# Projections and feed-forward products in four column tiles of the array

## The chip, the cores and the metric

The kernel runs on one core of a Trainium2 chip. The metric is device time in microseconds (us) per execution, taken as the median of several runs. All runs quoted here were fast, with a mean granted clock between 0.96 and 0.98. Two kernels that run in the same rounds on the same chip are compared by a ratio: the mean time of one kernel's fast runs over that of the other's of the same rounds, with a 95% interval, so it is not quite the ratio of the medians that stand beside it.

Engines in the profile are PE (TensorE matmul), PEld (TensorE weight load), DVE (VectorE), ACT (ScalarE), POOL (GpSimd) and SP (SyncE).

## The reference

Sixteen graphs of 1024 nodes with 128 features share one adjacency matrix. Each graph passes three transformer layers whose attention is masked by that matrix, and then one graph-attention layer. Everything is fp32. Cut to one layer:

```python
q, k, v = h @ Wq, h @ Wk, h @ Wv              # 8 heads of 16
s = einsum("bhqd,bhkd->bhqk", q, k) / 4
p = softmax(where(adj, s, -inf)) @ v
x1 = layer_norm(h + p @ Wo + bo)              # ln1
h  = layer_norm(x1 + relu(x1 @ W1 + b1) @ W2 + b2)   # ln2, W1 128x256, W2 256x128
```

## The kernel before

The unit of work is a block: one graph in one layer, 48 in all. A block is a row of 32 steps. In each step TensorE computes the scores of four heads for 128 keys and 512 queries, then the products of older exponentials with v, then at most one "piece" of other work: a transpose (T), a projection, or a feed-forward product. The order on TensorE is fixed by the program. The order on ACT, DVE and POOL is made by a scheduler when the program is built.

```python
def slot():   # scores: 3 x 2 banks of PSUM
    return psum.tile([P, N], dtype, tag="s", name="s", bufs=3)
def bank():   # every piece: one bank
    return psum.tile([P, 512], F32, tag="t", name="t", bufs=1)
sums = psum.tile([P, 512], F32, tag="acc", name="acc", bufs=1)   # products with v: one bank
...
def project(lhs, rhs, h, out):            # Wv, Wo, W2: N=128
    ps = bank()
    for t in range(4):
        for f in range(len(lhs)):
            nc.tensor.matmul(ps[:, t * P:(t + 1) * P], lhs[f][:, t * P:(t + 1) * P], rhs[f],
                             start=(f == 0), stop=(f == len(lhs) - 1))
    out(slice(4 * h, 4 * h + 4), ps)
...
def run():                                # split(): Wk, Wq, N=512
    ps = bank()
    nc.tensor.matmul(ps, w[n], s["xT", h], start=True, stop=True)
    with soon():
        nc.scalar.copy(hi[:, c], ps)
        nc.vector.tensor_sub(lo[:, c], ps, hi[:, c].bitcast(F32))
...
def run():                                # ffn1(): W1, N=512
    ps = bank()
    nc.tensor.matmul(ps, w["W1"][:, f * P:(f + 1) * P], s["x1T", h], start=True, stop=True)
    with soon():
        nc.scalar.activation(s["h", f, h], ps, AF.Relu, bias=w["b1"][:, f:f + 1], scale=1.0)
...
def score_step(step):                     # two pairs of heads
    for pp in range(2):
        ...                               # two row tiles, 64 rows each, into slot()
        on_pool = pp == 0 and kt not in BOTH_ON_DVE
        if on_pool:
            nc.scalar.activation(ev, psv, AF.Exp, scale=HD ** -0.5)
            nc.gpsimd.tensor_mul(ev, ev, m)
        else:
            nc.vector.tensor_add(ev, psv, m)
            nc.scalar.activation(ev, ev, AF.Exp, scale=HD ** -0.5)   # in place
...
def av_step(step, e, acc, first, last):   # four column tiles of 32, 17 columns used in each
    for j in range(J):
        nc.tensor.matmul(acc[j * SLOT:j * SLOT + HD + 1, :], v_bufs[m % 2][:, kt, 2 * j + g, :], e[:, j, :],
                         start=first, stop=last)
```

All eight PSUM banks are taken (six for scores, one for sums, one for pieces). Each piece must be copied out of its one bank, mostly by ACT, before the next piece may begin. ACT has two exponentials in each step besides.

Of the kernel before, what the change touches and what calls it, by code (L numbers as in the profile page):

```python
# [18 lines left out]
P = 128  # L19
# [4 lines left out]
SLOT = 32  # L24
# [24 lines left out]
def gnn_stack(tc: tile.TileContext, a: dict, out: bass.AP):  # L49


    nc = tc.nc
    with tc.tile_pool(name="flag", bufs=1) as fp:
        flag = fp.tile([1, 1], I32, name="flag")
        fast_path(tc, a, out, flag)
        bad = nc.values_load(flag[0:1, 0:1], min_val=0, max_val=1024)  # L56
        with tc.If(bad > 0):
            general_path(tc, a, out)
# [48 lines left out]
def fast_path(ctx: ExitStack, tc: tile.TileContext, a: dict, out: bass.AP, flag):  # L107
    nc = tc.nc
# [16 lines left out]
    def bank():  # L125

        return psum.tile([P, 512], F32, tag="t", name="t", bufs=1)

    def half_tile(name):

        return work.tile([P, 512], F32, tag="w", name=name, bufs=TILES["w"])
# [113 lines left out]
    for i in range(2):  # L245
        t = const.tile([P, NT, H, HD + 1], F32, name=f"v{i}")
# [4 lines left out]
    def soon():  # L251

        return tc.high_priority(offset=SOON)

    def transpose_half(name, src, h, gain=None, bias=None):

        dst = half_tile(name)
        ps = bank()
        for t in range(4):
            nc.tensor.transpose(ps[:, t * P:(t + 1) * P], src[:, 4 * h + t, :], identf)  # L260
        with soon():
            if gain is None:
                nc.scalar.copy(dst, ps)
            else:
                nc.scalar.activation(dst, ps, AF.Identity, scale=gain, bias=bias)
        return dst

    def v3(ps):
        return ps.rearrange("p (t d) -> p t d", d=D)

    def rows(v, n=NT):
        return v[:, None, :].to_broadcast([P, n, D])

    def project(lhs, rhs, h, out):

        ps = bank()
        for t in range(4):
            for f in range(len(lhs)):
                nc.tensor.matmul(ps[:, t * P:(t + 1) * P], lhs[f][:, t * P:(t + 1) * P], rhs[f],  # L279
                                 start=(f == 0), stop=(f == len(lhs) - 1))  # L280
        out(slice(4 * h, 4 * h + 4), ps)

    def with_stats(x):

        return (x, work.tile([P, NT, 6], F32, tag="st", name="st", bufs=4),
                work.tile([P, NT, 2], F32, tag="mv", name="mv", bufs=4))
# [8 lines left out]
    def add_and_stats(n):  # L295
        def out(ts, ps):
            with soon():
                nc.vector.tensor_add(n[0][:, ts, :], v3(ps), n[0][:, ts, :])  # L298
            stats(n, ts)
        return out  # L300

    def normalise(n, ts):

        z, _, mv = n
        m, v = mv[:, ts, 0], mv[:, ts, 1]
        nc.gpsimd.tensor_scalar(m, m, -1.0, None, op0=OP.mult)  # L306
        nc.gpsimd.tensor_scalar(v, v, EPS, None, op0=OP.add)
        nc.gpsimd.tensor_tensor(v, v, half_neg[:, ts], OP.pow)  # L308
        for t in range(ts.start, ts.stop):
            nc.gpsimd.tensor_scalar(z[:, t, :], z[:, t, :], mv[:, t, 0:1], mv[:, t, 1:2], op0=OP.add, op1=OP.mult)  # L310

    def scale_shift(z, gain, bias):
        n = z.shape[1]
        nc.gpsimd.tensor_mul(z, z, rows(gain, n))  # L314
        nc.gpsimd.tensor_add(z, z, rows(bias, n))  # L315
# [3 lines left out]
    def check_range(r):  # L319

        for k, op in enumerate((OP.min, OP.max)):
            nc.vector.tensor_reduce(chk[:, k, checks[0]:checks[0] + 1].bitcast(I32), r.bitcast(I32), AX.X, op)
        checks[0] += 1


    def proj_tasks(m):
        b, l = blocks[m]
        w = W[l]
        s = {}

        def t0(h):
            def run():
                x = state["x", b]
                if l == 0:
                    s["xT", h] = transpose_half("xT", x, h)
                    if h == 1:
                        nc.gpsimd.tensor_add(x, x, rows(w["bo"]))
                else:

                    s["xT", h] = transpose_half("xT", x, h, W[l - 1]["ln2_gc"], W[l - 1]["ln2_bc"])  # L340
                    if h == 1:
                        scale_shift(x, W[l - 1]["ln2_g"], w["bo"])
            return run

        def split(n, h):
            def run():
                if h == 0:
                    state[n, m] = [work.tile([P, N], F32R, tag="hl", name=i, bufs=4) for i in ("hi", "lo")]
                hi, lo = state[n, m]
                c = slice(h * 512, (h + 1) * 512)  # L350
                ps = bank()
                nc.tensor.matmul(ps, w[n], s["xT", h], start=True, stop=True)
                with soon():
                    nc.scalar.copy(hi[:, c], ps)
                    nc.vector.tensor_sub(lo[:, c], ps, hi[:, c].bitcast(F32))  # L355
            return run

        def v(h):
            def out(ts, ps):
                with soon():  # L360
                    nc.scalar.copy(v_bufs[m % 2][:, ts].rearrange("p t h s -> p (t h) s")[:, :, :HD],
                                   ps.rearrange("p (m d) -> p m d", d=HD))
            return lambda: project([s["xT", h]], [w["Wv"]], h, out)

        pieces = [t0(0), t0(1), split("Wk", 0), split("Wk", 1), split("Wq", 0), split("Wq", 1), v(0), v(1)]
        return [(2 if n in (3, 4, 5, 6) else 1, f, {0: "+w", 1: "+w", 6: "-w", 7: "-w"}.get(n, "")) for n, f in enumerate(pieces)]
# [59 lines left out]
    def post_tasks(b, l):  # L426
        w = W[l]
        s = {}
        att, recs = state["A"], state["recs"]

        def gather(h):
            def run():
                s["aT", h] = half_tile("aT")
                nc.vector.transpose(s["aT", h], att[:, h].rearrange("p k g d -> p (k g d)"))
                if h == 1:
                    check_range(recs.rearrange("p g h k -> p (g h k)"))
            return run

        def out_proj(h):
            def run():  # L440
                if h == 0:
                    s["n1"] = with_stats(state["x", b])
                project([s["aT", h]], [w["Wo"]], h, add_and_stats(s["n1"]))
                normalise(s["n1"], slice(4 * h, 4 * h + 4))
            return run

        def x1t(h, alone=False):
            def run():
                x1 = s["n1"][0]
                s["x1T", h] = transpose_half("x1T", x1, h, w["ln1_gc"], w["ln1_bc"])  # L450
                if alone:
                    scale_shift(x1[:, 4 * h:4 * h + 4, :], w["ln1_g"], w["b2"])
                elif h == 1:
                    scale_shift(x1, w["ln1_g"], w["b2"])
            return run

        def ffn1(f, h):
            def run():
                s["h", f, h] = half_tile("hT")
                ps = bank()  # L460
                nc.tensor.matmul(ps, w["W1"][:, f * P:(f + 1) * P], s["x1T", h], start=True, stop=True)  # L461
                with soon():
                    nc.scalar.activation(s["h", f, h], ps, AF.Relu, bias=w["b1"][:, f:f + 1], scale=1.0)  # L463
            return run

        def ffn2(h):
            def run():
                if h == 0:
                    s["n2"] = with_stats(state["x", b])
                project([s["h", f, h] for f in range(NF)], [w["W2"][:, f, :] for f in range(NF)], h,  # L470
                        add_and_stats(s["n2"]))
                normalise(s["n2"], slice(4 * h, 4 * h + 4))
            return run

        def both():
            gather(0)()
            gather(1)()


        together = [(2, both, "+w +w"), (1, out_proj(0), "-w"), (1, out_proj(1), "-w"), (5, x1t(0), "+w"), (1, x1t(1), "+w")]  # L480
        for h in range(2):
            together += [(1, ffn1(0, h), "+w"), (1, ffn1(1, h), "+w -w")]
        together += [(1, ffn2(0), "-w -w"), (1, ffn2(1), "-w -w")]
        alone = [[(1, gather(h), "+w"), (1, out_proj(h), "-w"), (3, x1t(h, True), "+w"), (1, ffn1(0, h), "+w"),
                  (1, ffn1(1, h), "+w -w"), (1, ffn2(h), "-w -w")] for h in range(2)]
        return together, alone
# [211 lines left out]
    n = 0  # L698
# [47 lines left out]
    ps = bank()  # L746
# [226 lines left out]
```

## Time and profile before

| | before |
|---|---|
| median of 3 runs | 4299.87 us (4289.3 to 4303.16) |
| profiled span, clock | 4307.9 us, 0.974 |
| busy: PE, DVE, ACT, POOL | 93%, 79%, 79%, 80% |
| matmul records | 26069 (an fp32 product has two) |
| an ordinary block | 77.45 us |
| a block beside a graph's last layer | 84 to 109 us |

"An ordinary block" is measured from the first scores of a block to those of the next. In a timeline, a bracket is idle time and what ended it.

The prediction shows the page's lines and TensorE's timeline. Two further views matter. The first is the timeline of ACT in the kernel before, over the two steps whose TensorE rows the prediction shows (start in us, duration, line, operation, operands; a bracket is idle time and what ended it):

```profile
3654.59 1.05 ACT L401 ACTIVATE e<-e 128x1024 f32<-128x1024 f32 x1
3655.54 1.01 ACT L397 ACTIVATE e<-s 128x1024 f32<-128x1024 f32 x1
3656.44 1.06 ACT L401 ACTIVATE e<-e 128x1024 f32<-128x1024 f32 x1
3657.39 0.69 ACT L463 ACTIVATE hT<-t,b 128x512 f32<-128x512 f32 x1
```

The piece of L461 that began at 3655.54 leaves its bank through the copy hT at L463. Between that piece and its copy, ACT runs exponentials 0.90 to 0.95 us apart, and the copy ends at about 3658.1. TensorE wants the bank again at 3658.24, when the next piece begins. The copy is hidden, with little to spare.

The second view is the list of waits of the kernel before (waiter, released by, total us, times, longest us):

```profile
PEld s L390 <- ACT e L397: 202.8, 242, 1.7
...
PE s L390 <- ACT e L397: 54.8, 120, 1.4
```

Scores wait for the exponential that reads their PSUM slot. A wait of PEld may be hidden behind a matmul that still runs; a wait of PE is idle time.

### The profile page before, as it was taken

How to read it: one execution, taken by the hardware profiler on the slowest of the kernel's cores; microseconds unless marked ns; L12 is line 12 of the kernel's file. 1: busy time of each engine (PE TensorE's matmuls, PEld its weight loads, DVE VectorE, ACT ScalarE, POOL GpSimd, SP SyncE). 2: the span in 40 equal slices, each digit the busy share in tenths (PEclk: the TensorE clock that was granted, in tenths of full speed). 3: DMA queues.
4: the chain of work that ended last, by engine and by line, in shares of the span. 5: the costliest groups of instructions: out<-in, count | busy, mean ns of one | idle time of the engine just before them, and what ended most of it. 6: DMA issues, size and time to landing. Idle time of an engine off the chain costs nothing. (4 is left out here: it accounts for less than half of the span.)

```text
span 4307.9 us, 70734 instructions
## 1 busy us (share of the span) xinstructions
PE 4005.4 (93%) x26069; PEld 1631.7 (38%) x26069; DVE 3408.0 (79%) x5324; ACT 3408.3 (79%) x3961; POOL 3442.0 (80%) x3010
## 2 busy tenths in 40 slices
PE   7999999999999999999999999999999999999996
PEld 2333333344443333334444333333344433333445
DVE  6888878877777888877777787887777788888774
ACT  7898989866767988987676898997776689898660
POOL 4788888876779888887677988887777788888784
PEclk9999999999999999999999999999999999999997
DMA  5222122221111222121112222221211212221100
GB/s 145 64 60 54 49 57 59 58 52 50 43 50 47 60 59 52 49 58 50 50 43 57 56 51 53 60 59 40 60 46 45 64 40 60 59 55 44 45 21 17
DMA packets 126147, 230.77 MB, mean 54 GB/s; under 512 B 36705, under 2 KB 75617, under 8 KB 125793
## 3 DMA queue, kind: packets, MB, share of 16 engines
q1 hardware_dynamic: 122896, 225.14, 20.9%
q8 instruction: 209, 3.42, 0.3%
q10 hardware_dynamic: 2896, 1.01, 0.1%
q14 instruction: 146, 1.19, 0.1%
HBM read 15.54 MB, written 8.39 MB: 6 GB/s over the span
## 5 line engine op out<-in xcount | busy, mean ns | idle before, releaser
L400 DVE TENSOR_TENSOR e<-s,mask_add 128x1024 f32<-128x1024 f32 x2112 | 2503.1, 1212 | 505.6 <-PE s L390 393.0
L401 ACT ACTIVATE e<-e 128x1024 f32<-128x1024 f32 x2112 | 2194.4, 1060 | 428.9 <-DVE e L400 415.3
L398 POOL TENSOR_TENSOR e<-e,mask 128x1024 f32<-128x1024 f32 x960 | 2047.3, 2145 | 470.2 <-ACT e L397 454.2
L407 PE MATMUL acc<-e,v 128*17 128x512 f32 x12288 | 1645.0, 607 | 44.9 <-POOL e L398 32.0
L390 PE MATMUL s<-Wq,Wk 64*128 64x512 f32 x6144 | 1217.0, 461 | 126.5 <-ACT e L397 54.8
L397 ACT ACTIVATE e<-s 128x1024 f32<-128x1024 f32 x960 | 979.8, 1021 | 137.8 <-PE s L390 73.6
L390 PEld LDWEIGHTS s<-Wq,Wk 64*128 64x128 f32 x6144 | 500.6, 186 | 1036.9 <-DVE e L400 330.9
L407 PEld LDWEIGHTS acc<-e,v 128*17 128x17 f32 x12288 | 206.5, 95 | 559.7 <-issue 440.6
L310 POOL TENSOR_SCALAR x<-x,mv 128x128 f32<-128x128 f32 x896 | 389.2, 447 | 22.7
L314 POOL TENSOR_TENSOR x<-x,ln_g 128x1024 f32<-128x1024 f32 (+1 forms) x97 | 228.8, 2359 | 129.8 <-PE t L260 118.9
L576 PEld LDWEIGHTS t<-hd,e 128*128 128x128 f32 x2048 | 259.3, 208 | 67.2 <-issue 31.8
L576 PE MATMUL t<-hd,e 128*128 128x129 f32 x2048 | 271.4, 295 | 7.8 <-DVE x L582 3.5
L308 POOL TENSOR_TENSOR mv<-mv,half_neg 128x4 f32<-128x4 f32 x224 | 232.0, 1036 | 18.3
L298 DVE TENSOR_TENSOR x<-t,x 128x512 f32<-128x512 f32 x192 | 132.1, 688 | 123.3 <-PE t L279 118.9
L461 PE MATMUL t<-x1T,W 128*128 128x512 f32 x384 | 217.7, 649 | 5.1 <-DVE x L582 1.0
L279 PEld LDWEIGHTS t<-W,hT 128*128 128x128 f32 x1536 | 183.9, 196 | 88.0 <-ACT hT L463 35.8
L279 PE MATMUL t<-W,hT 128*128 128x128 f32 x1536 | 202.5, 286 | 3.4 <-DVE lo L355 2.4
L291 DVE BATCH_NORM_STATS2 st<-x 128x6 f32<-128x128 f32 x896 | 197.3, 279 | 2.7
L260 PE MATMUL t<-identf,x 128*128 128x128 f32 x896 | 151.8, 294 | 36.5 <-DVE lo L355 25.5
L260 PEld LDWEIGHTS t<-identf,x 128*128 128x128 f32 x896 | 97.1, 144 | 230.7 <-DVE lo L355 55.8
L306 POOL TENSOR_SCALAR mv<-mv 128x4 f32<-128x4 f32 x224 | 52.8, 236 | 140.0 <-DVE mv L293 101.8
L463 ACT ACTIVATE hT<-t,b 128x512 f32<-128x512 f32 x192 | 132.2, 688 | 40.8 <-PE t L461 40.0
(83 smaller groups left out, 2588.0 us busy)
## 6 DMA issues: line engine op xcount, KB each, us to landing
Wk<-hi SPq DMA_DIRECT2D x384, 128.0 KB
Wk<-lo SPq DMA_DIRECT2D x384, 128.0 KB
Wq<-hi SPq DMA_DIRECT2D x384, 128.0 KB
Wq<-lo SPq DMA_DIRECT2D x384, 128.0 KB
x<-in_x_dram SPq DMA_DIRECT2D x16, 512.0 KB
out_dram<-x SPq DMA_DIRECT2D x31, 256.0 KB
ai<-in_adj_dram SPq DMA_DIRECT2D x8, 512.0 KB
g_rows<-parts SPq DMA_DIRECT2D x124, 4.0 KB
```

The costliest lines, as they stand in the source:

```text
L260: nc.tensor.transpose(ps[:, t * P:(t + 1) * P], src[:, 4 * h + t, :], identf)
L279: nc.tensor.matmul(ps[:, t * P:(t + 1) * P], lhs[f][:, t * P:(t + 1) * P], rhs[f], start=(f == 0), stop=(f == len(lhs) - 1))
L308: nc.gpsimd.tensor_tensor(v, v, half_neg[:, ts], OP.pow)
L310: nc.gpsimd.tensor_scalar(z[:, t, :], z[:, t, :], mv[:, t, 0:1], mv[:, t, 1:2], op0=OP.add, op1=OP.mult)
L314: nc.gpsimd.tensor_mul(z, z, rows(gain, n))
L390: nc.tensor.matmul(ps[:, r * 512:(r + 1) * 512], k[64 * r:64 * r + 64, kt * P:(kt + 1) * P], q[64 * r:64 * r + 64, q0:q0 + 512], start=Tru ...
L397: nc.scalar.activation(ev, psv, AF.Exp, scale=HD ** -0.5)
L398: nc.gpsimd.tensor_mul(ev, ev, m)
L400: nc.vector.tensor_add(ev, psv, m)
L401: nc.scalar.activation(ev, ev, AF.Exp, scale=HD ** -0.5)
L407: nc.tensor.matmul(acc[j * SLOT:j * SLOT + HD + 1, :], v_bufs[m % 2][:, kt, 2 * j + g, :], e[:, j, :], start=first, stop=last)
L576: nc.tensor.matmul(ps[:, i * (D + 1):(i + 1) * (D + 1)], e[:, t, i * P:(i + 1) * P], s["hd"][t // 4][:, t % 4, :], start=(t == 0), stop=(t ...
```

## The change

Scores use two row tiles of the array, products with v use four column tiles, and pieces used the whole array. The change gives the pieces the shape of the products with v that stand ahead of them, so that one change of shape per piece falls away. It costs three more matmul instructions for each one split. Nothing else in the program text changes.

```diff
+    def by_columns(dst, lhsT, rhs, start=True, stop=True):
+        for j in range(0, P, SLOT):
+            nc.tensor.matmul(dst[j:j + SLOT, :], lhsT[:, j:j + SLOT], rhs, start=start, stop=stop)
@@ project
-                nc.tensor.matmul(ps[:, t * P:(t + 1) * P], lhs[f][:, t * P:(t + 1) * P], rhs[f],
-                                 start=(f == 0), stop=(f == len(lhs) - 1))
+                by_columns(ps[:, t * P:(t + 1) * P], lhs[f][:, t * P:(t + 1) * P], rhs[f],
+                           start=(f == 0), stop=(f == len(lhs) - 1))
@@ split
-                nc.tensor.matmul(ps, w[n], s["xT", h], start=True, stop=True)
+                by_columns(ps, w[n], s["xT", h])
@@ ffn1
-                nc.tensor.matmul(ps, w["W1"][:, f * P:(f + 1) * P], s["x1T", h], start=True, stop=True)
+                by_columns(ps, w["W1"][:, f * P:(f + 1) * P], s["x1T", h])
```

## The prediction

> **What bounds the kernel now.** I read four views, in this order: the page (busy shares and costliest groups), the timeline of TensorE over a few steps, the table of busy time by stretch, and the waits.
>
> The page first: its first line, and rows of the costliest groups (line, engine, operation, shapes, count | busy us, mean ns | idle before).
>
> ```profile
> PE 4005.4 (93%) x26069; PEld 1631.7 (38%) x26069; DVE 3408.0 (79%) x5324; ACT 3408.3 (79%) x3961; POOL 3442.0 (80%) x3010
> ...
> L407 PE MATMUL acc<-e,v 128*17 128x512 f32 x12288 | 1645.0, 607 | 44.9 <-POOL e L398 32.0
> L390 PE MATMUL s<-Wq,Wk 64*128 64x512 f32 x6144 | 1217.0, 461 | 126.5 <-ACT e L397 54.8
> ...
> L461 PE MATMUL t<-x1T,W 128*128 128x512 f32 x384 | 217.7, 649 | 5.1 <-DVE x L582 1.0
> L279 PE MATMUL t<-W,hT 128*128 128x128 f32 x1536 | 202.5, 286 | 3.4 <-DVE lo L355 2.4
> ```
>
> TensorE is busy 93% and the others about 80%. Its stationary shapes are the point: scores are 64*128 (two row tiles), products with v are 128*17 (four column tiles), projections and feed-forward are 128*128 (whole array). One step of the loop is scores, then products with v, then at most one "piece" (a projection, a feed-forward product or a transpose). Every fp32 product has two records, so eight records at L407 are four products. The timeline shows one step after the other (start, duration, records):
>
> ```profile
> 3655.54 1.12 PE L461 MATMUL t<-x1T,W 128*128 128x512 f32 x2
> 3656.60 0.73 PE L390 MATMUL s<-Wq,Wk 64*128 64x512 f32 x4
> 3657.26 1.05 PE L407 MATMUL acc<-e,v 128*17 128x512 f32 x8
> 3658.24 1.12 PE L461 MATMUL t<-x1T,W 128*128 128x512 f32 x2
> 3659.30 0.73 PE L390 MATMUL s<-Wq,Wk 64*128 64x512 f32 x4
> 3659.96 1.05 PE L407 MATMUL acc<-e,v 128*17 128x512 f32 x8
> 3660.94 2.05 PE L279 MATMUL t<-W,hT 128*128 128x128 f32 x16
> 3662.93 0.74 PE L390 MATMUL s<-Wq,Wk 64*128 64x512 f32 x4
> ...
> 4190.78 1.91 PE L407 MATMUL acc<-e,v 128*17 128x512 f32 x16
> 4192.62 0.74 PE L564 MATMUL s<-g_rows,h_rows 4*128 4x256 f32 x8
> ```
>
> Read starts, not durations (ends are modelled). No brackets follow these rows: TensorE waits for nobody. Products with v and an L461 piece take 3656.60 - 3654.56 = 2.04 us together (the L407 before the first row starts at 3654.56). At 4190 the trace has the one place where two groups of products with v follow each other: 1.84 us, although both pairs stream the same columns. The 0.20 us is what changing the shape of the array costs. In the single records (starts a few ns apart) it is two terms: after the last L407 matmul the next shape starts 522 ns later, where the two rounds of the double group are 429 ns apart, so about 95 ns of emptying; and the first weight load of the new shape is exposed, some 107 ns (the first L279 matmul to the second is 214 ns, later ones 112).
>
> The table by stretch, for the 77 us of one block in a part without the last layer:
>
> ```profile
> 3591.00:3614.00 23.00, 21.35 (x146) 6.08 (x145) 22.50 (x34) 22.61 (x24) 21.06 (x21) 1.00 0.36 92
> 3614.00:3668.00 54.00, 52.23 (x336) 20.11 (x335) 42.31 (x65) 47.08 (x55) 45.47 (x36) 1.00 0.17 40
> ```
>
> Columns: PE, PEld, DVE, ACT, POOL busy. In the 23 us without pieces ACT (98%) and DVE bind; in the 54 us with pieces TensorE does (97%), ACT is at 87%. All changed work lies in the second stretch, so there a saving on TensorE counts.
>
> **What the Trainium skill says.** "TensorEngine Tiling (Array Packing)", Key Properties: changing the tiling mode, not merely the tile, drains TensorE, and different tiles load weights and multiply in parallel. The trace agrees: 95 ns between shapes, none in the double group. Same page, Restrictions: column tiling excludes Fast Weight Load. "TensorE: Matmul & The Clock Gate", Weight-path perf modes, says that load is not used for fp32, so nothing is lost here. The latter page, Part 1, gives a floor of about 25 ns between matmul starts. Four column tiles at N=128 need one start per 27 ns, close to it. The trace shows L407 tiles starting 6 to 7 ns apart, which speaks for no such limit between tiles, though only for bursts of eight.
>
> **The change, part by part.** Each 128*128 product becomes four 128*32 ones writing four quarters of the output partitions, all streaming the same operand. Removed: one change of shape per piece. Added: from 3072 records at L279 and 768 at L352 and L461 three times as many again, 11520 more matmuls and as many loads (26069 becomes 37589). Moved: nothing in the data flow; transposes, scores and L524, L576 stay.
>
> N=512 pieces: now 2.04 us from the products with v to the next scores, then as the double group 1.84: -0.20. N=128, eight records: now 2.07 (products with v start at 1066.98, the next scores at 1069.05); then two rounds of 429 ns, eight rounds of 112 ns (four tiles at once, so a round lasts as long as one matmul now), 20 ns of stagger, 98 ns of emptying: 1.87, again -0.20. Sixteen records: now 2.97 (3659.96 to 3662.93), then 858 + 16 x 112 + 118 = 2.77: -0.20. The change back to scores stays in all.
>
> Number of pieces, from the page's counts: L279 with Wv 768/8 = 96, with Wo 96, with W2 1536/16 = 96, L352 384/2 = 192, L461 192: 672. 672 x 0.20 = **134 us** of TensorE.
>
> What comes off it:
> - Pieces that wait anyway. The waits list DVE lo 74.1 us in 45 times and several ACT and DVE waits before L279 and L461; I take 90 pieces as late, where emptying was hidden and about 0.12 us is lost: -11.
> - The instruction order of both kernels shows that the scheduler, which counts in instructions, moves PSUM copies on ACT: of 672 or so, about 120 stand one exponential later (48 of 96 v copies, 30 x1T, 28 xT), 30 one earlier. One exponential is about 0.95 us, and there is one bank for all pieces, needed again after about 1.65 us. I estimate 0.15 us of new wait for 90 net cases: -13.
> - ACT goes from 87% to 47.08/51.3 = 92% in the stretch with pieces, so some of the gain is lost to its queue, an estimate: -10.
>
> 134 - 34 = 100 us: 4300 - 100 = **4200 us**, 2.3% less.
>
> **The rivals.**
> 1. Small products don't keep the pace. If a round of four at N=128 took 150 ns instead of 112 (weight loads of four tiles in a row, 4 x 27 ns, or issue), the 384 groups of eight rounds would pay 384 x 8 x 38 ns = 117 us, and the change would be a wash, about 4310. At 200 ns a round it would be 4450. For it: 64 or 128 instructions must pass in 0.9 or 1.8 us where now it is 16 or 32. Against it: the loads in the double group start 1 to 2 ns after the matmul ahead of them and are hidden, and 32 columns load faster than 128 (L407 loads of 17 columns show 95 ns, of 128 columns 190). About 12%.
> 2. ACT and DVE take over as the bound. In the stretch without pieces they already do; if ACT held every piece step, with two exponentials (1.9 us) and a copy (0.6) against TensorE's new 2.50, half of the gain would stay: 4235. For it: 98% in the first stretch. Against it: not every piece has a copy on ACT, and steps in the last-layer phases, where ACT is near 70%, run at TensorE's pace too.
> 3. Full gain with 107 ns rounds (the streaming time of 128 fp32 columns, 427/4) instead of 112: 384 x 8 x 5 ns = 15 us more, nothing lost elsewhere: 4150.
>
> **Range and chances.** Rival 1 makes the upper tail, rival 2 puts weight between 4215 and 4250, rival 3 ends the lower side. The 2% line is 4214. Range 4150 to 4265; faster 0.63, same 0.32, slower 0.05.
>
> **What would show it.** Right: products with v to scores over an L461 piece at 1.84 us, over eight-round pieces near 1.87, over sixteen-round near 2.77; 37589 matmul records; TensorE's wait for ACT and DVE up some 20 to 40 us; the stretch with pieces some 2.5 us shorter per block, the one without unchanged. Wrong: rounds of small products well above 112 ns (rival 1), new idle time before pieces or scores put down to ACT copies (rival 2), or a remaining gap between products with v and pieces, which would mean that 17 and 32 columns are not one shape.

## More of the kernel before

By the trace, 22 of the 48 blocks take 77.2 to 77.8 us, most of them 77.45. Most of the others run beside the graph-attention layer of a graph that has just finished.

## The result, and the profile after

The changed kernel is correct and takes 4254.32 us (4 runs, 4250.95 to 4260.73) against 4301.51 us of the kernel before (4 runs, 4289.3 to 4308.17). The ratio is 0.9895, interval 0.987 to 0.9921: 1.05% faster, or 47 us. The forecast gain was 100 us.

The page of the changed kernel, its first line and three rows of the costliest groups:

```profile
PE 3892.9 (92%) x37589; PEld 1575.2 (37%) x37589; DVE 3404.9 (80%) x5324; ACT 3417.3 (80%) x3961; POOL 3451.4 (81%) x3010
...
L412 PE MATMUL acc<-e,v 128*17 128x512 f32 x12288 | 1635.4, 604 | 56.5 <-DVE tt L423 29.8
...
L271 PE MATMUL t<-x1T,W 128*32 128x512 f32 x1536 | 206.2, 609 | 18.0 <-ACT hT L468 8.6
...
L271 PE MATMUL t<-W,hT 128*32 128x128 f32 x6144 | 187.1, 274 | 9.1 <-DVE x L303 5.2
```

The pieces are now of shape 128*32, with four times the records, 37589 in all as forecast. TensorE is busy 112 us less. The idle time just before the W1 pieces went from 5.1 us to 18.0. That is the first sign that the pieces now come sooner than their bank is free.

From the single records, the span between the last product with v and the next scores fell where nobody waits as follows. With N=512 it fell from 1578 ns to 1381, with eight rounds (Wv and Wo) from 1610 to 1396, and with sixteen (W2) from 2504 to 2269. The gap from products with v to the piece went from 522 ns to 409, and the first weight load of the piece is hidden. Multiplied by 384, 192 and 96 pieces, that is 75.6 + 41.1 + 22.6 = **139 us** that TensorE no longer needs, or 2.9 us per block. So the part that was to happen on TensorE did happen, a little better than the 134 us forecast.

The table of busy time by stretch of the changed kernel (PE, PEld, DVE, ACT, POOL busy), over the same block that the prediction shows of before:

```profile
3547.50:3570.50 23.00, 21.55 (x152) 6.17 (x152) 22.48 (x32) 22.27 (x24) 21.61 (x21) 1.00 0.39 93
3570.50:3624.20 53.70, 50.49 (x580) 19.26 (x572) 42.33 (x66) 47.78 (x55) 45.23 (x36) 1.00 0.16 41
```

The stretch without pieces is unchanged at 23 us. The stretch with pieces is 53.7 us long where it was 54.0, although TensorE's busy time in it fell by 1.7 us and TensorE needs 2.9 us less. An ordinary block takes 77.15 us where it took 77.45. So the ordinary blocks give back nearly all of their gain: 22 x 0.30, about 7 us of the 47, where TensorE's need fell by 22 x 2.9 = 64. The other blocks gave the rest (two of them: 102.03 to 98.40, and 103.23 to 98.46).

Two rows of the waits of the changed kernel, those that answer to the ones shown of before:

```profile
PEld s L395 <- ACT e L402: 237.2, 313, 1.5
...
PE s L395 <- ACT e L402: 67.9, 138, 0.9
```

TensorE's waits for the exponentials grew. Counted over the whole trace as the time between matmul starts beyond the smallest spacing of its kind, all waits of TensorE grew from 480 to 566 us, while the sum of smallest spacings fell by 140. A second count of the records finds the same growth of 86 us; 56 of it lie before pieces and transposes, 19 before products with v.

Where this happens is best seen in two places of the same ordinary block. The first is the steps of W1. TensorE's timeline in the changed kernel:

```profile
3612.37 1.04 PE L271 MATMUL t<-x1T,W 128*32 128x512 f32 x8
3613.34 0.74 PE L395 MATMUL s<-Wq,Wk 64*128 64x512 f32 x4
3614.01 1.05 PE L412 MATMUL acc<-e,v 128*17 128x512 f32 x8
3615.28 1.06 PE L271 MATMUL t<-x1T,W 128*32 128x512 f32 x8 [0.21 <-ACT hT L468]
```

ACT's timeline over the same step:

```profile
3611.74 1.05 ACT L406 ACTIVATE e<-e 128x1024 f32<-128x1024 f32 x1
3612.69 1.01 ACT L402 ACTIVATE e<-s 128x1024 f32<-128x1024 f32 x1
3613.59 1.05 ACT L406 ACTIVATE e<-e 128x1024 f32<-128x1024 f32 x1
3614.54 0.68 ACT L468 ACTIVATE hT<-t,b 128x512 f32<-128x512 f32 x1
```

ACT does what it did before: exponentials 0.90 to 0.95 us apart, then the copy, which begins 2.17 us after its piece here and 1.85 us in the rows of before. The piece of 3612.37 could be followed by the next after 2.50 us, at 3614.87, but its copy begins at 3614.54 and ends past 3615.1. So the next piece begins at 3615.28 and takes the first weight load in the open again. A copy that was just hidden in a step of 2.70 us is not hidden in one of 2.50.

The second place is DVE's order around the sums of the products with v. First DVE's timeline in the kernel before:

```profile
3625.89 0.69 DVE L298 TENSOR_TENSOR x<-t,x 128x512 f32<-128x512 f32 x1
...
3627.41 0.30 DVE L293 BATCH_NORM_AGGREGATE mv<-st 128x2 f32<-128x6 f32 x3
3627.62 0.68 DVE L418 STREAM_TRANSPOSE tt<-acc 128x512 f32<-128x512 f32 x1
```

DVE's timeline at the same step of the changed kernel:

```profile
3582.91 0.69 DVE L303 TENSOR_TENSOR x<-t,x 128x512 f32<-128x512 f32 x1 [0.16 <-PE t L271]
...
3584.70 1.19 DVE L405 TENSOR_TENSOR e<-s,mask_add 128x1024 f32<-128x1024 f32 x1
3585.81 0.71 DVE L423 STREAM_TRANSPOSE tt<-acc 128x512 f32<-128x512 f32 x1
```

The row of TensorE's timeline in the changed kernel that waits for it:

```profile
3586.66 1.05 PE L412 MATMUL acc<-e,v 128*17 128x512 f32 x8 [0.65 <-DVE tt L423]
```

In the kernel before, the transposition that frees the bank of sums starts 1.73 us after the addition at L298. In the changed kernel the scheduler has put a masked addition ahead of it, and it starts 2.90 us after. The products with v at 3586.66 waited for it: that step takes 2.36 us instead of 1.65. The program text of DVE is the same in both kernels; only its order differs. Between the orders of the two built programs 406 places differ on ACT, 364 on DVE and 255 on POOL.

### The profile page after: what moved, and what is told of

It is laid out like the page before. It is cut to its first block, busy times and chain, and to the rows that moved or that the text cites. A ratio compares the mean times of both kernels' runs of the same rounds, so it can differ in the third digit from the quotient of the medians.

```text
span 4253.7 us, 93788 instructions
## 1 busy us (share of the span) xinstructions
PE 3892.9 (92%) x37589; PEld 1575.2 (37%) x37589; DVE 3404.9 (80%) x5324; ACT 3417.3 (80%) x3961; POOL 3451.4 (81%) x3010
## 4 chain that ended last, share of the span: by engine, by line
PE 37%; DVE 26%; ACT 23%; issue 7%; POOL 5%; DMA 1%; SPq 1%; DVEq 0%; ACTq 0%; POOLq 0%
DVE e L405 16%; ACT e L406 13%; PE t L271 11%; PE acc L412 10%; PE s L395 9%; ACT e L402 6%; PE t L581 6%; DVE st L296 2%; POOL e L403 2%; DVE tt L423 1%; DVE e L572 1%; DVE x L303 1%; PE t L260 1%; ACT xT L265 1%; DVE lo L360 1%
## 5 line engine op out<-in xcount | busy, mean ns | idle before, releaser
L271 PE MATMUL t<-x1T,W 128*32 128x512 f32 x1536 | 206.2, 609 | 18.0 <-ACT hT L468 8.6
L271 PEld LDWEIGHTS t<-W,hT 128*32 128x32 f32 x6144 | 172.0, 111 | 70.6 <-issue 32.9
L271 PE MATMUL t<-W,hT 128*32 128x128 f32 x6144 | 187.1, 274 | 9.1 <-DVE x L303 5.2
```

The source lines that it names most:

```text
L271: nc.tensor.matmul(dst[j:j + SLOT, :], lhsT[:, j:j + SLOT], rhs, start=start, stop=stop)
```

## The experiments

The account to settle: TensorE needs 139 us less and 47 came through. Theories: (a) the new order of ACT, DVE and POOL costs it; (b) ACT's copies, which stand behind exponentials, hold the bank; (c) DVE or POOL do; (d) the small products do not keep pace in some of the places. A "pair" below is a kernel with whole products and one with column tiles, alike otherwise, and its worth is the difference of the two. The column tiles alone gave 47 us. All runs have three rounds.

### The two sizes of products apart

`only_512` leaves the N=128 products whole, and `only_128` leaves the N=512 products whole:

```diff
 only_512, in project:
-                by_columns(ps[:, t * P:(t + 1) * P], lhs[f][:, t * P:(t + 1) * P], rhs[f], ...)
+                nc.tensor.matmul(ps[:, t * P:(t + 1) * P], lhs[f][:, t * P:(t + 1) * P], rhs[f], ...)
 only_128, in split and ffn1 (one of two):
-                by_columns(ps, w[n], s["xT", h])
+                nc.tensor.matmul(ps, w[n], s["xT", h], start=True, stop=True)
```

> Column tiles only for the N=512 products (Wq, Wk, W1: 384 pieces), whole array for the N=128 ones. On TensorE alone these pieces save 384 x 0.196 = 75 us of the 139 us. If the gain is lost wherever ACT copies out a piece (all 384 of these are copied by ACT), this run shows little: 0 to 20 us faster than before. If the loss is spread evenly over all pieces, a bit over half of the 47 us: 25 us.

> Column tiles only for the N=128 products (Wv, Wo, W2: 288 pieces), which save 192 x 0.214 + 96 x 0.236 = 64 us on TensorE. If the gain is lost at pieces with an ACT copy, this run keeps most of what Wo and W2 save (about 45 us) and reaches 30 to 45 us. If the loss is spread evenly: 22 us.

Measured against 4299.85 us: `only_512` 4266.41 us, ratio 0.9921 (0.9898 to 0.9945), correct. `only_128` 4300.82 us, ratio 1.0004 (0.9983 to 1.0025), correct. By TensorE's need they were to save 75 and 64 us; they saved 34 and nothing. Neither run fits its expectations: `only_512` is above both figures and `only_128` below both. By the names of operations and tiles in the traces, `only_512` has almost the order of before (26 places differ on ACT), while `only_128` has a shifted one (321). An ordinary block takes 76.78 and 78.05 us. This speaks for (a), but does not separate it from what the two sizes do.

### A lighter ACT, order free

The in-place exponentials were done on 416 of 512 columns, in both kernels. Their outputs are wrong, and the flag for the general path is held at 0 (it is in all kernels with wrong outputs but the two with a lighter DVE, which do not touch it).

```diff
-                nc.scalar.activation(ev, ev, AF.Exp, scale=HD ** -0.5)
+                nc.scalar.activation(ev[:, :, :416], ev[:, :, :416], AF.Exp, scale=HD ** -0.5)
...
-    nc.vector.tensor_add(flag, both[:, 0:1], both[:, 1:2])
+    nc.vector.tensor_scalar(flag, both[:, 0:1], 0.0, None, op0=OP.mult)
```

> Wrong result on purpose: the whole-array kernel with every in-place exponential cut from 512 to 416 of 512 columns, which takes some 330 us (10%) off ACT. It is the reference for the next run. If ACT sets part of the pace already, 60 to 120 us faster than before; if TensorE alone does, under 30.

> The same cut with column tiles. Theory (the gain went to ACT, whose two exponentials and a copy last as long as the shortened step): with ACT 10% lighter the change is worth 110 us or more against the whole-array kernel with the same cut. Rival (DVE, POOL or the order of instructions took it): still 40 to 70 us.

Measured: 4264.0 us (0.9916, 0.9897 to 0.9936) and 4213.0 us (0.9807, 0.9788 to 0.9825). The pair is worth 51 us, where the plain pair is worth 47. That is no restoration and fits the rival, so the first form of (b) looked wrong. But the scheduler had made a new order for each kernel, so two things had moved at once. From here on the order had to be held.

### The order exchanged

Each kernel was given the other's order on ACT, DVE and POOL. A stored list names the order, and each two neighbours get an ordering edge, which adds no semaphore. TensorE's order is the program's in all.

```diff
+def keep_order(tc, nc):
+    ...                                     # ORDER: the other kernel's order
+    for engine in (Activation, DVE, Pool):
+        mine = [i for i in nc.cur_bb.bb.instructions if i.engine == engine]
+        ...
+        for a, b in zip(rank, rank[1:]):
+            tc.add_manual_dep(mine[b], mine[a].name, DependencyInfo(NoSync, DATA), reason="order")
```

> Column tiles as in the changed kernel, but ACT, DVE and POOL are held to the order of instructions of the kernel before (which the change had shifted: 406, 364 and 255 places differ). Theory of order: the gain that is missing went to copies and sums that now stand one place later, so this run gets it back: 90 us or more faster than before (4210 or less). Rival (engine load or the one bank, whatever the order): within 15 us of the changed kernel, about 4254.

> The kernel before with the order of ACT, DVE and POOL that the scheduler made for the changed kernel. Theory of order: 40 to 60 us slower than before (about 4350). Rival: within 15 us of before.

Measured against 4302.0 us:

| | order of before | order of after |
|---|---|---|
| whole products | 4302 us; block 77.45 | 4313.89 us (1.0036, 1.0015 to 1.0057); block 78.41 |
| column tiles | 4234.43 us (0.9851, 0.983 to 0.9873); block 76.10 | 4254.32 us; block 77.15 |

Both kernels are correct. The order of after costs 12 us with whole products and 20 us with column tiles. (The 4254.32 is from the rounds of the result; by the two ratios to the kernel before, 0.9895 and 0.9851, the 20 us are known to some 14 us either way. The traces show that all three engines keep the order given.) So (a) is shown, at about 20 of the 92 missing us. That is far less than was expected of it: `cols_old_order` was to reach 4210 by the theory of order and to stay above 4239 by its rival, and it lies between; the 12 us of `whole_new_order` fit the rival. The step that waited for DVE's transposition is back at 1.65 us. Column tiles in the order of before are worth 68 us, so 139 - 68 = 71 us are still missing.

Here it is ACT that is seen to hold the bank. TensorE in the W1 steps of `cols_old_order`:

```profile
3586.36 1.04 PE L302 MATMUL t<-x1T,W 128*32 128x512 f32 x8
...
3589.51 1.06 PE L302 MATMUL t<-x1T,W 128*32 128x512 f32 x8 [0.46 <-ACT hT L499]
```

The step takes 3.15 us instead of 2.50.

### A lighter DVE

DVE lost the masked additions of the first pair in two of eight steps (384 of 1.21 us). Their exponentials read the scores directly, and the outputs are wrong.

```diff
+            if pp == 0 and kt in (2, 7):
+                nc.scalar.activation(ev, psv, AF.Exp, scale=HD ** -0.5)
-            if on_pool:
+            elif on_pool:
```

> Wrong result on purpose: in two of eight steps the first pair's masked addition on DVE is left out (the exponential reads the scores straight from PSUM): 384 fewer additions of 1.21 us, 465 us or 14% of DVE. Reference for the next run. If DVE sets part of the pace: over 60 us faster than before.

> The same with column tiles. Theory of order: about the 47 us of the plain pair remain (30 to 70 us against the whole-array kernel with the same cut). Rival (DVE took the gain): 110 us or more.

Measured: 4369.89 us (1.0172) and 4346.95 us (1.0112). Both are slower than the kernel before, though 465 us of work went from DVE; the pair is worth 23 us. The experiment is inconclusive. It changed the order, and it changed which engine holds the scores' slot. Why they are slower stays open, and of DVE the runs say nothing.

### Copies earlier, and pieces further apart

If copies come one exponential too late, one can move them: 355 of 480 copies (hT, v, hi) were put one in-place exponential earlier on ACT, in the held order. Or one can space the pieces, so that no piece needs the bank after one step.

```diff
 early: the stored order of ACT, with 355 exchanges of a copy and the exponential ahead of it
 spread:
-        return [(2 if n in (3, 4, 5, 6) else 1, f, ...) for n, f in enumerate(pieces)]
+        return [(2 if n else 1, f, ...) for n, f in enumerate(pieces)]
-        together = [..., (1, out_proj(1), "-w"), (5, x1t(0), "+w"), (1, x1t(1), "+w")]
+        together = [..., (2, out_proj(1), "-w"), (5, x1t(0), "+w"), (2, x1t(1), "+w")]
-            together += [(1, ffn1(0, h), "+w"), (1, ffn1(1, h), "+w -w")]
+            together += [(2, ffn1(0, h), "+w"), (2, ffn1(1, h), "+w -w")]
-        together += [(1, ffn2(0), "-w -w"), (1, ffn2(1), "-w -w")]
+        together += [(2, ffn2(0), "-w -w"), (2, ffn2(1), "-w -w")]
-                    if at == 6:
+                    if at == 0:
```

> The kernel before, its order of DVE and POOL kept, and on ACT 355 of the 480 copies of relu, v and hi moved one in-place exponential earlier. Theory of the one bank (a piece waits until ACT, behind its exponentials, has copied the last piece out of the only bank): 10 to 40 us faster than before. Rival (total load of an engine): within 10 us of before.

> The same order with column tiles. Theory of the one bank: the change is then worth more than with the old order (4234): 90 us or more against the whole-array kernel of the same order. Rival: the pair stays at 65 us or below.

> The kernel before with its pieces spread over the whole block: the projections start at step 0 of a block and not at 6, and pieces of one chain keep two steps apart, so nearly every piece is followed by a step without one. The order of all engines is the scheduler's own. Theory (the packed stretch, where each step has a piece, an ACT copy and the one bank, is where time is lost): 50 to 150 us faster than before. Rival (engine loads): within 40 us.

> The same spread with column tiles. Theory: copies have a spare step, so TensorE's saving of 139 us comes through nearly whole: 100 us or more against the whole-array kernel with the same spread. Rival (ACT, DVE or POOL load takes it whatever the spacing): 30 to 65 us, as in the plain pair or with the old order.

Measured against 4303.5 us, all correct: `whole_early` 4327.1 us (1.0054, 1.0031 to 1.0077), `cols_early` 4258.59 us (0.9902, 0.9885 to 0.992), `whole_spread` 4444.91 us (1.0328, 1.0307 to 1.0348), `cols_spread` 4409.53 us (1.0254, 1.0227 to 1.0281). Earlier copies cost 24 us in both kernels (against 4303.5 and 4234.43), and the pair is worth 69 us, as much as without them. So the place of these copies among the exponentials is no cure, and both expectations of a gain failed. With column tiles the wait only moved: by the list of waits TensorE waits 4.1 us for hT before pieces where it was 15.4, and 14.3 us for the copy x1T where it was 0.8. Spread pieces are slower still. There the share of POOL's mask products in the chain that ended last is 8.9%, where it is 2% after the change. The pair is worth 35 us. This experiment may test POOL's queue more than the bank; it gives the spacing of pieces no support and does not settle it.

### A much lighter ACT or POOL, order held

With the order of before held in all six kernels, the in-place exponentials (ACT), the mask products (POOL), or both were done on half of their columns. Outputs are wrong.

```diff
 acthalf, bothhalf:
-                nc.scalar.activation(ev, ev, AF.Exp, scale=HD ** -0.5)
+                nc.scalar.activation(ev[:, :, :256], ev[:, :, :256], AF.Exp, scale=HD ** -0.5)
 poolhalf, bothhalf:
-                nc.gpsimd.tensor_mul(ev, ev, m)
+                nc.gpsimd.tensor_mul(ev[:, :, :256], ev[:, :, :256], m[:, :, :256])
```

> Wrong result on purpose: the order of before held, in-place exponentials on half the columns (about 0.43 us less for each of 2112, some 900 us off ACT). Reference for the next run. Where ACT sets the pace: over 100 us faster than before; else under 60.

> The same with column tiles. Theory ACT: 110 us or more against its whole-array twin. Rival (POOL, DVE or the hand-over): 60 to 80 us, as with the full exponentials and the old order (67 us).

> Wrong result on purpose: the order of before held, mask products on POOL on half the columns (about 1.05 us less for each of 960, some 1000 us off POOL). Reference for the next run. Where POOL sets the pace: over 60 us faster than before; else under 30.

> The same with column tiles. Theory POOL: 110 us or more against its whole-array twin. Rival (ACT, DVE or the hand-over): 60 to 80 us.

> Whole products, order of before held, in-place exponentials on ACT and mask products on POOL both cut to half of their columns (wrong outputs on purpose). It is the base for the columns version. ACT alone cut gave a ratio of 0.990 and POOL alone 0.991; expected about 0.985, near 4240 us.

> Column tiles, order of before held, both cuts. With ACT alone cut the column tiles gave 105 of the 139 us that TensorE saves. If POOL takes its turn once ACT is out of the way, the pair gives 115 to 139 us. If what is missing is DVE's subtraction that frees the bank, and the hand-overs between the engines, POOL's cut changes nothing: 100 to 110 us.

Measured, with the kernel before at 4302.58 us for the first four and 4304.45 us for the last two:

| cut | whole products | column tiles | pair | ordinary block |
|---|---|---|---|---|
| none, order held | 4302.0 | 4234.43 (0.9851) | 68 us | 77.45 to 76.10 |
| POOL | 4264.5 (0.991) | 4197.82 (0.9753) | 67 us | 77.45 to 76.10 |
| ACT | 4260.72 (0.9903) | 4155.97 (0.9657) | 105 us | 76.57 to 74.51 |
| ACT and POOL | 4222.15 (0.982) | 4118.85 (0.9577) | 103 us | 76.56 to 74.41 |

The half widths of the ratios' intervals are about 0.002, and up to 0.003 in the last row. ACT's in-place exponentials cut in half bring 37 us of the 71 back, known to some 15 us either way from the intervals; 105 us is just short of the 110 expected of the theory. POOL brings nothing, neither alone nor behind ACT. That the 37 us were lost at the bank, and not at the scores' slots, is seen in the lines of TensorE's W1 pieces (busy, mean ns, then idle time and what ended it), of `cols_old_order` and then of `acthalf_cols`:

```profile
L302 PE MATMUL t<-x1T,W 128*32 128x512 f32 x1536 | 204.0, 603 | 20.0 <-ACT hT L499 15.4 <-DVE x L618 1.0 <-ACT xT L296 0.9
L302 PE MATMUL t<-x1T,W 128*32 128x512 f32 x1536 | 202.6, 599 | 2.3 <-DVE x L618 1.0 <-ACT xT L296 0.9 <-DVE parts L580 0.3
```

Counted from the single records as above, TensorE's waits before all pieces and transposes grow by 30 us from whole products to column tiles in the order of before (88 to 118), and not at all with ACT cut (73 and 73). So (b) is shown, for about 30 of the 37 us, and POOL is out of (c). ACT is busy 63% in `acthalf_cols`, and its W1 steps show how. TensorE's timeline in `acthalf_cols`:

```profile
3524.89 1.04 PE L302 MATMUL t<-x1T,W 128*32 128x512 f32 x8
...
3527.39 1.04 PE L302 MATMUL t<-x1T,W 128*32 128x512 f32 x8
```

ACT's timeline over the same step:

```profile
3524.60 1.01 ACT L433 ACTIVATE e<-s 128x1024 f32<-128x1024 f32 x1
3525.51 0.63 ACT L437 ACTIVATE e<-e 128x512 f32<-128x512 f32 x1
3526.03 0.69 ACT L499 ACTIVATE hT<-t,b 128x512 f32<-128x512 f32 x1
```

The copy now begins 1.14 us after the piece and not 2.17 as in the changed kernel. (In `cols_old_order`, the twin with full exponentials, the first W1 copy begins 2.40 us after its piece.) All four W1 steps take 2.50 us, with no bracket.

The steps of one ordinary block, from the first scores to the next scores in us, by the trace of each kernel:

| step, piece | before | after | cols_old_order | acthalf_cols | bothhalf_cols |
|---|---|---|---|---|---|
| 8, T | 2.35 | 2.57 | 2.59 | 2.49 | 2.49 |
| 9, Wk | 2.80 | 2.94 | 2.59 | 2.51 | 2.51 |
| 10, Wo | 3.61 | 3.62 | 3.62 | 3.62 | 3.62 |
| 12, none | 1.65 | 2.36 | 1.65 | 1.65 | 1.65 |
| 15, Wq | 2.95 | 3.41 | 2.81 | 2.75 | 2.96 |
| 16, T | 3.24 | 2.23 | 3.30 | 3.30 | 3.30 |
| 20, W1 | 2.70 | 2.95 | 2.50 | 2.50 | 2.50 |
| 21, W1 | 2.82 | 2.50 | 3.18 | 2.51 | 2.51 |
| 23, W1 | 2.70 | 2.93 | 2.76 | 2.50 | 2.51 |
| 24, W2 | 3.62 | 3.39 | 3.39 | 3.39 | 3.40 |

From the order of after to that of before, steps 9, 12, 15 and 20 get shorter and 16 and 21 longer. With ACT cut, 21 and 23 come back. With both out of the way, steps 8, 10, 15 and 16 are left. Against `bothhalf_whole` (2.28, 3.61, 2.94 and 3.24) they take 0.21, 0.01, 0.02 and 0.06 us more, where two of them were to gain 0.2 each. That is 0.7 us per ordinary block, or 22 x 0.7, about 16 us, of the 139 - 105 = 34 us that are open. The other half lies in the other blocks, whose steps were not looked at. At step 8 the next scores wait 0.18 us for an exponential of ACT that stands behind the copy xT, so ACT is not wholly out of the way. TensorE's timeline at steps 10 and 16 of `bothhalf_cols`:

```profile
3462.12 1.08 PE L302 MATMUL t<-Wo,aT 128*32 128x128 f32 x32 [0.89 <-DVE lo L391]
...
3477.14 0.63 PE L291 MATMUL t<-identf,x 128*128 128x128 f32 x4 [1.03 <-DVE lo L391]
```

DVE's timeline at step 10:

```profile
3460.15 1.22 DVE L436 TENSOR_TENSOR e<-s,mask_add 128x1024 f32<-128x1024 f32 x1 [1.08 <-PE s L426]
3461.29 0.68 DVE L391 TENSOR_TENSOR lo<-t,hi 128x512 fp32r<-128x512 f32 x1
```

At both places the bank is freed by DVE's subtraction lo, which stands behind a masked addition. TensorE comes sooner and waits longer. That this is DVE's order and not its load is argued from these rows, not shown. DVE was idle for 1.08 us before that addition, waiting for TensorE's scores, which speaks against its load; but no run moved lo ahead of the addition, and the one pair that lightened DVE was inconclusive.

## Why the prediction was wrong

- **The saving on TensorE** was right: 139 us of need against 134. The three spans that were to show it, 1.84, 1.87 and 2.77 us, are 1.84, 1.85 and 2.73 by the starts in the timeline, and rounds of four N=128 products take 109 to 110 ns. (One term was misread, without effect on the sum: by the prediction's own starts the exposed load is 214 - 112 = 102 ns, not 107.) Rival 1 is refuted; so is theory (d).
- **The deductions** were the failed step: "134 - 34 = 100 us". The 34 us measured 139 - 47 = 92 us: about 20 for the order, 37 for ACT, and 34 that stay open.
- **"ACT goes from 87% to 47.08/51.3 = 92% ... -10"** is the term furthest off. By the pair with ACT's in-place exponentials cut in half it is about -37. The share over the stretch is the wrong measure. A step with a copy hT or x1T holds two exponentials, 0.90 to 0.95 us from start to start, and a copy of 0.57 to 0.67: 2.4 to 2.6 us on ACT against TensorE's new 2.50. In those steps ACT is nearly as long as TensorE, and because the pieces have one bank, each copy that comes late is a wait. The prediction had this sum in rival 2 and gave it too little weight. Rival 2's time was 4235; the order held gave 4234 and the order of after 4254, since rival 2 had no cost for the order. That 4234 meets 4235 is partly luck: rival 2 put all of the loss down to ACT, and ACT has 37 of these 71 us.
- **"I estimate 0.15 us of new wait for 90 net cases: -13"** measured about -20 with column tiles (12 with whole products). The prediction counted copies on ACT only, and counted them rightly (48 v, 30 x1T and 28 xT copies are later in the trace). The dearest single place was DVE's transposition behind a masked addition, 0.71 us in a step. Its reason, that the scheduler counts in instructions, is tested by no run here.
- **"I take 90 pieces as late ... -11"** was too small. What stays after ACT and POOL are relieved is 34 to 36 us. In an ordinary block it lies at four steps, two of which wait for DVE's lo. At the one of them with a split product, step 10, the saving does not shrink to 0.08 us, as assumed; it is lost whole (3.61 to 3.62). The cause beyond that is open.
- **"The stretch with pieces some 2.5 us shorter per block"**: 0.3 us was measured. "TensorE's wait for ACT and DVE up some 20 to 40 us": its waits of all kinds are up 86.
- The skill's page "TensorEngine Tiling (Array Packing)", Performance Considerations, PSUM Bottleneck, says that tiling speeds up TensorE but not the evacuation of PSUM, whose copies may become the bottleneck, and advises to use both ScalarE and VectorE for it. The prediction read that page and left this out. The runs agree: 37 us by ACT. Its advice needs care here, for DVE's lo holds the bank too (waits of 0.89 and 1.03 us in the rows of `bothhalf_cols`).

The best correct kernel found is `cols_old_order`: 4234.43 us, 1.5% faster than before, and 20 us below the changed kernel in medians of different rounds.

## What to carry to other kernels

Before crediting a faster TensorE, sum for one step what each engine that frees its buffer must do in that step, in the order of its queue, and compare with TensorE's new length; a share over a stretch of 54 us hides the wait. Where a scheduler orders the other engines, hold their order when a change is judged, or compare the two orders by runs: here the order alone was worth 20 us of a 68 us gain. Neighbouring products should share one shape of the array, which was worth 0.20 to 0.24 us per change of shape removed here, wherever nothing else waited.

## What the Trainium skill lacked or had wrong

- "TensorEngine Tiling (Array Packing)", Key Properties: it says that a change of mode drains TensorE, but not what that costs. Here it was 522 - 409 = 113 ns from the last product with v to the next piece, and with the first weight load in the open 197 to 235 ns per piece.
- The same page, Instruction Overhead, warns of about 60 cycles of overhead for each matmul and does not say what becomes of it when four column tiles run side by side. Here 32 and 64 records of N=128 in four column tiles kept 109 to 110 ns per round of four, where one whole product took 112, so the quadrupled count cost nothing.
- "TensorE: Matmul & The Clock Gate", Part 1: a floor of about 25 ns from start to start, said without an exception for tiles. Between different column tiles this trace has starts mostly 5 to 9 ns apart within a round (Part 3 of the same page has about 4 ns from tile to tile); over whole rounds it has four in 109 to 110 ns, which does not contradict the floor as a mean.
- "TensorEngine Tiling (Array Packing)", PSUM Bottleneck, is right in direction, but gives no way to tell when it sets in. Here it did with ACT at 80% of the span, because two exponentials and one copy (2.4 to 2.6 us) met a step of 2.50 us and one bank.
- No page has it that a change on TensorE alone moves the instructions of the other engines when a scheduler orders them: 406, 364 and 255 places on ACT, DVE and POOL here, for 20 us.
